# A selective-scan and attention block: when its weights are loaded, and when its scans begin

## The chip, the cores and the metric

The kernel runs on one core of a Trainium2 chip. The metric is device time in microseconds of one execution, the median of three runs. PE is TensorE (matmuls and transposes), DVE VectorE, ACT ScalarE, POOL GpSimd. SP is SyncE; it issues every transfer of this kernel, one after the other, from one in-order queue. Each engine works through its own instruction list in order and waits at an instruction until what it needs is there.

## The reference

Eight images of 64 x 64 positions and 96 channels go through two layers. The first normalises the image in groups of channels, projects it to 2 x 192 channels, convolves one half with 3 x 3 taps per channel, and scans it along two families of diagonals, forwards and backwards (four directions), with 16 states per channel:

```
xz = x @ in_proj_w.T;  xh, z = split(xz)
xc = silu(depthwise_conv3x3(xh) + conv_b)
xs = stack([xc[diag], xc[anti], xc[diag] reversed, xc[anti] reversed])
dts, B, C = split(x_proj_weight @ xs)
delta = softplus(dt_projs_weight @ dts + dt_projs_bias)
A = -exp(A_logs)
h = h * exp(delta * A) + (delta * u) * B      # one step per position
y = h . C + Ds * u
out = layernorm(y) * silu(z) @ out_proj_w.T
```

The second layer adds an attention without a softmax (so that keys times values can be summed first) and a two-layer perceptron whose operands are rounded to an 8-bit float. The decay `A` comes from `A_logs`, one logarithm for each direction, channel and state: 4 x 192 x 16 numbers.

## The kernel before, in words

`weights` loads and prepares all weights. The convolution and the projection before it are folded into one set of weights `wf`: the half of `w_in` is transposed on PE, multiplied by each of nine taps on DVE, transposed back on PE and copied into `wf` (lines 154 to 168, twice nine taps). `a_neg` holds the decays with channels on the partitions: line 145 fetches each run of eight channels transposed, out of an array that has eight channels times 16 states on 128 partitions, 96 transfers in all. `wx` and `ws` (lines 130, 136, 138) hold the weights of B, C and delta, in small pieces; `skip`, `pick` and `xb` are constants built on DVE. The rest serves the later layers. All this stands before `run`.

`run` prepares an image and scans it. Preparing has these parts:

- `measures` (line 379): eight chunks `xt` are loaded (`fetched`, line 366), turned on PE (line 375), and their statistics taken on DVE (line 389); an aggregate follows.
- `front` (line 425): `norm` loads and turns the chunks again and writes the normalised image `xp` on ACT; `convolve` makes each of eight pieces with four or five times 9 matmuls on PE (line 493; the trace has two records for each) and z with two more (line 500), applies silu on ACT and stores `gate` and `image` (lines 512 and 519). Then `walk` (line 529) reads each of eight pieces of the scan order out of `image` with 12 transfers (`ut`, line 538), turns them on PE (line 545), copies them on ACT (line 547) and stores them as `seq` (line 550, two transfers). Three walks run at a time.
- `bring` (line 897) loads a piece `u` of `seq`, and `prologue` (line 820) computes from it delta, delta times u, and B and C, in a chain over PE, ACT, POOL, DVE and PE again (lines 835 to 893). The rows of C go to DRAM (`crow`, line 851) and come back broadcast (`cc`, line 914).

Then the scan loop runs: 8 images x 16 pieces x 16 states = 2048 steps. A step is a decay on ACT (line 923), a feed made on ACT or DVE and PE (lines 937, 945, 947, 962), three scans on DVE (line 958), a product with C on POOL (line 979) and sums on PE (line 993). Line 974 copies the carry once per step.

Beside the loop a planner (`Work`, line 225) lays other work into it. Jobs are Python generators that yield the engine they want and an estimated time; in each step `at` lets jobs go on as far as a credit per engine allows. `SPIN` is a yield that costs nothing and lasts one round. `finish` (line 326) lays down rounds of jobs alone, without a credit, until a condition holds. Jobs need PSUM banks: two are always theirs, and the three `feed` banks as well while no scan runs. All of this decides the order of instructions at build time; nothing of it runs on the chip.

For image 0 the order was: weights; `measures(0)`, `front(0)` and `measures(1)` alone until all are done (line 1065); two `bring`; `prologue(0)` alone; then the loop. At step 5 of image b the planner finishes what is left alone, and then starts `between(b)`, which is `front(b + 1)` and the end layers of image b - 1; at step 128 it starts `measures(b + 2)`.

Of the kernel before, what the change touches and what calls it, by code (L numbers as in the profile page):

```python
# [17 lines left out]
P = 128  # L18
HH = WW = 64
L = HH * WW  # L20
DM = 96
# [29 lines left out]
@with_exitstack  # L51
def hybrid_block(ctx, tc, x, out, w):


    nc = tc.nc
    NB = x.shape[0]
    const = ctx.enter_context(tc.tile_pool(name="const", bufs=1))
    dram = ctx.enter_context(tc.tile_pool(name="dram", bufs=4, space=DRAM))
    k = weights(tc, const, w)
    pool = ctx.enter_context(tc.tile_pool(name="scan", bufs=1))  # L60
    psum = ctx.enter_context(tc.tile_pool(name="psum", bufs=1, space=PSUM))
    with tc.manual_schedule():

        k.tables = lambda: nc.scalar.preload_act_table_set("natural_log_exp_and_others")
        run(tc, pool, psum, dram, x, out, k, NB)


def weights(tc, const, w):


    nc = tc.nc
# [8 lines left out]

    k = SimpleNamespace()
    k.ident = load("ident", [P, P], w["c_ident"])
    k.group = load("group", [DM, DM], w["c_group"])
    k.heads = load("heads", [DM, DM], w["c_heads"])
    k.last = load("last", [1, DM + 1], w["c_last"])
    k.w_in = load("w_in", [DM, 2 * DI], w["w_in"])
    k.w_kv = load("w_kv", [DM + 1, 2 * DM], w["w_kv"])
    k.w_qT = load("w_qT", [DM, DM + 1], w["w_qT"])
    k.w_ff = load("w_ff", [DM, DM], w["w_ff"])
    k.b_ff = load("b_ff", [1, DM], w["b_ff"])  # L90
    k.eps = tile("eps", [P, 1])
    nc.vector.memset(k.eps, 1e-5)
    k.one = tile("one", [P, 1])
# [10 lines left out]
    k.w2q = tile("w2q", [P, 3, DM], F8)  # L104
    k.b1q = tile("b1q", [P, 3])
    k.b2q = tile("b2q", [P, 4, DM])
    nc.gpsimd.memset(k.wf, 0.0)
    nc.gpsimd.memset(k.wx, 0.0)
    nc.gpsimd.memset(k.ws, 0.0)

    k.pick = tile("pick", [NX, FEED.count("D"), P])
    for j, n in enumerate(n for n in range(NS) if FEED[n] == "D"):
        for d in range(2):
            at = XB + d * NS + n
            nc.vector.tensor_copy(
                k.pick[:, j, d * GC : (d + 1) * GC], k.ident[0:NX, at : at + 1].to_broadcast([NX, GC])
            )

    nc.vector.tensor_copy(k.xb, k.ident[0:NX, 2 * NR : 2 * NR + 1])
    with nc.allow_non_contiguous_dma(reason="weights, once"), tc.tile_pool(  # L120
        name="prep", bufs=1
    ) as prep, tc.tile_pool(name="prep2", bufs=2) as prep2, tc.tile_pool(
        name="prepp", bufs=2, space=PSUM
    ) as pp:
        dd = tile("dd", [P, 2, G], pool=prep)
        for d in range(2):
            for g, a, lo, hi, at in PIECES:
                rows = slice(d * GC + at, d * GC + at + hi - lo)
                for first, n, name in ((0, NR, "w_dt"), (XB, NS, "w_b"), (XC, NS, "w_c")):
                    nc.sync.dma_start(  # L130
                        out=k.wx[rows, :, g, first + d * n : first + (d + 1) * n], in_=w[name][lo:hi, a, d::2, :]
                    )
                nc.sync.dma_start(out=dd[rows, :, g], in_=w["ds"][lo:hi, a, d::2])
                for q in range(2):
                    bias = w["b_step"][lo:hi, 2 * q + d, a : a + 1].rearrange("i o -> o i")
                    nc.sync.dma_start(out=k.ws[2 * NR : 2 * NR + 1, q, g, rows], in_=bias)
            for q in range(2):
                nc.sync.dma_start(
                    out=k.ws[d * NR : (d + 1) * NR, q, :, d * GC : (d + 1) * GC],
                    in_=w["w_step"][:, 2 * q + d, :].rearrange("r (g i) -> r g i", i=GC),  # L140
                )
                logs = w["a_logs"][:, 2 * q + d, :].rearrange("(i n) j -> j i n", n=NS)
                for j in range(NJ):
                    lo = d * GC + j % (GC // DPT) * DPT
                    nc.sync.dma_start(out=k.a_neg[lo : lo + DPT, q, j // (GC // DPT), :], in_=logs[j])
        nc.scalar.activation(k.a_neg, k.a_neg, AF.Exp)
        nc.vector.tensor_scalar(k.a_neg, k.a_neg, -1.0, None, ALU.mult)

        both = tile("both", [P, G], pool=prep)
        nc.vector.tensor_tensor(both, dd[:, 0, :], dd[:, 1, :], ALU.add)  # L150
        for g in range(G):
            nc.vector.tensor_scalar(k.skip[:, g, :], k.ident, both[:, g : g + 1], None, ALU.mult)

        conv_w = load("conv_w", [HC, 2, 9], w["conv_w"], pool=prep)
        for a in range(2):
            nc.sync.dma_start(
                out=k.wf[DM : DM + 1, 4, a * HC : (a + 1) * HC], in_=w["conv_b"][:, a : a + 1].rearrange("p o -> o p")
            )
            ps = pp.tile([HC, DM], F32, tag="ps", name="ps")
            nc.tensor.transpose(ps, k.w_in[:, a * HC : (a + 1) * HC], k.ident[:DM, :DM])  # L160
            turned = prep2.tile([HC, DM], F32, tag="turned", name="turned")
            nc.vector.tensor_copy(turned, ps)
            for i in range(9):
                tap = prep2.tile([HC, DM], F32, tag="tap", name="tap")
                nc.vector.tensor_scalar(tap, turned, conv_w[:, a, i : i + 1], None, ALU.mult)
                ps = pp.tile([DM, HC], F32, tag="ps", name="ps")
                nc.tensor.transpose(ps, tap, k.ident[:HC, :HC])
                nc.vector.tensor_copy(k.wf[0:DM, i, a * HC : (a + 1) * HC], ps)

        w_out = load("w_out", [HC, 2, DM], w["w_out"], pool=prep)  # L170
        ln_w = load("ln_w", [HC, 2], w["ln_w"], pool=prep)
        ln_b = load("ln_b", [HC, 2], w["ln_b"], pool=prep)
        for a in range(2):
            nc.vector.tensor_scalar(k.w_ln[:, a, :], w_out[:, a, :], ln_w[:, a : a + 1], None, ALU.mult)
            nc.vector.tensor_scalar(k.b_ln[:, a, :], w_out[:, a, :], ln_b[:, a : a + 1], None, ALU.mult)

        s = load("w1s", [DM, HID], w["w1"], pool=prep)
        nc.vector.tensor_copy(k.w1q, s, saturate=False)
        s = load("w2s", [P, 3, DM], w["w2"], pool=prep)
        nc.vector.tensor_copy(k.w2q, s, saturate=False)  # L180
        s = load("b1s", [P, 3], w["b1"], pool=prep)
        s8 = tile("b1e", [P, 3], F8, prep)
        nc.vector.tensor_copy(s8, s, saturate=False)
        nc.vector.tensor_copy(k.b1q, s8)
        s = tile("b2s", [P, 4, DM], pool=prep)
        nc.sync.dma_start(out=s, in_=w["b2"].unsqueeze(1).to_broadcast([P, 4, DM]))
        s8 = tile("b2e", [P, 4, DM], F8, prep)
        nc.vector.tensor_copy(s8, s, saturate=False)
        nc.vector.tensor_copy(k.b2q, s8)
    return k  # L190


# [32 lines left out]
class Work:  # L225
# [6 lines left out]
    def __init__(self, banks):  # L232
        self.now = 0
        self.alone = False
        self.urgent, self.jobs, self.streams = [], [], []
        self.free = [(b, -9) for b in banks]
        self.long = []
        self.credit = dict.fromkeys(self.PLACES, 0.0)

# [19 lines left out]
    def bank_for(self, j, place):  # L259
        if j not in self.urgent and not self.alone:  # L260
            if any(u.tag == "P" and u.bank for u in self.urgent) or j.bank == "long" and self.long:
                return None
        for i, (b, when) in enumerate(self.free):
            if when < self.now or place == 2 or self.alone:
                if j.bank == "long":
                    self.long.append(b)
                return self.free.pop(i)[0]
        return None
# [513 lines left out]
def run(tc, pool, psum, dram, x, out, w, NB):  # L782
# [269 lines left out]

    def first():
        yield from before(0)
        yield from begin(0)
        if NB > 1:
            yield from before(1)

    def all_done():
        return not (work.streams or work.jobs)  # L1060
# [1 line left out]

    w.tables()
    work.stream(first())
    work.finish(all_done)
    for m in range(2):
        bring(m)
    work.start(prologue(0), urgent=True)
    work.finish(lambda: not work.urgent)
    work.free = [f for f in work.free if any(f[0] is b for b in banks)]  # L1070

    work.start(prologue(1), urgent=True)
# [14 lines left out]
    for i in range(total + LAG + 1):  # L1087
        m, n = divmod(i, NS)
        b, at = divmod(i, PER)
        if i < total:  # L1090
            if at == LAG + 1:
                work.finish(all_done)
                work.stream(between(b))
            if at == PER // 2 and b + 2 < NB:
# [28 lines left out]
            fetch(i + 4)  # L1123
        feeds.pop(i, None)
    work.free += [(f, -9) for f in feed]
    work.stream(end(NB - 1))
    work.finish(all_done)

# [76 lines left out]
```

## Time and profile before

| what | value |
|---|---|
| median of three runs | 12146.02 us (12140.42 to 12148.66) |
| profiled execution, its time | 12157.04 us |
| its span, first to last instruction | 12155.1 us |
| PE, DVE, ACT, POOL busy | 82%, 80%, 78%, 80% |
| DMA queue of SP: packets, MB | 1137510, 1201.51 |
| first carry copy of the first step | 449.38 us after the start |
| 256 steps of image 0, from first carry to first carry | 1296.8 us |
| the same for image 1 | 1447.7 us |

Times in the timeline count from the start of the span. A row of it gives the start, the busy time, the engine, the line, the operation, the tile written and the tiles read, and the number of instructions merged into the row; in brackets the idle time before it and what ended it. SPq rows are issues of transfers, so their duration is the time of issue, waits between the merged ones included, and not that of the data. In the rows of windows each engine has its busy time and instruction count, then come the clock that PE was granted, the busy share of the DMA engines and GB/s.

### The profile page before, as it was taken

Reading aid. Unit: us, or ns where it says so; the run is one execution under the profiler, and the core shown is the slowest. Engines: PE = TensorE matmul, PEld = TensorE weight load, DVE = VectorE, ACT = ScalarE, POOL = GpSimd, SP = SyncE. Lnnn points to the kernel's source line nnn. Section 1 sums busy time; section 2 is a strip of 40 time slices with the busy share of each in tenths; the row PEclk is TensorE's granted clock in tenths of the full one; section 3 lists DMA queues with packets and bytes.
Section 4 is the critical chain, followed back from the end, with each engine's and each line's share of the span. In section 5 each row is a group of like instructions: output and inputs, shape, how many; then the busy total and the mean of one; then the engine's idle time right before and its main releaser. Section 6 shows DMA issues by size and latency. Waiting matters only on the chain.

```text
span 12155.1 us, 187007 instructions
## 1 busy us (share of the span) xinstructions
PE 9958.7 (82%) x62804; PEld 8012.1 (66%) x62804; DVE 9683.1 (80%) x11092; ACT 9501.2 (78%) x19842; POOL 9737.6 (80%) x6927
## 2 busy tenths in 40 slices
PE   4698889888898888988888888988889888888874
PEld 3476667666676666766677666766667666666653
DVE  1488998878888888888888888888888878888971
ACT  1588888877888788877888878887788878878862
POOL 0588998878988788888888889888898888889972
PEclk9799999998998989989899999999989899988985
DMA  2334333533335433353333433344333443322331
GB/s 53 91 92 124 100 93 94 136 104 96 94 88 134 112 94 93 90 141 101 95 90 106 127 102 95 90 127 117 92 92 93 132 108 93 100 87 84 100 93 42
DMA packets 1138471, 1213.47 MB, mean 100 GB/s; under 512 B 464998, under 2 KB 744167, under 8 KB 1137511
## 3 DMA queue, kind: packets, MB, share of 16 engines
q1 hardware_dynamic: 1137510, 1201.51, 36.0%
q8 instruction: 499, 8.18, 0.3%
q14 instruction: 462, 3.78, 0.1%
HBM read 877.94 MB, written 323.09 MB: 99 GB/s over the span
## 4 chain that ended last, share of the span: by engine, by line
PE 29%; ACT 22%; DVE 20%; POOL 11%; issue 9%; SPq 4%; DMA 4%; DVEq 0%; POOLq 0%; ACTq 0%
DVE h L958 13%; ACT feedT L937 8%; PE y L993 7%; PE feed L945 7%; ACT decay L923 6%; POOL h L979 6%; DVE feed L962 4%; PE bank L493 3%; DMA cc<-crow 2%; PE bank L835 2%; SPq L538 2%; PE bank L877 1%; POOL delta L874 1%; PE feed L947 1%; PE bank L858 1%
## 5 line engine op out<-in xcount | busy, mean ns | idle before, releaser
L979 POOL TENSOR_TENSOR h<-h,cc 128x1536 f32<-128x1536 f32 x2048 | 7073.1, 3454 | 401.7 <-DMA cc<-crow 205.0
L958 DVE TENSOR_TENSOR_SCAN h<-decay,carry,feed 128x512 f32<-128x512 f32 x5376 | 6500.6, 1261 | 623.0 <-PE feed L945 510.4
L923 ACT ACTIVATE decay<-delta,a_neg 128x512 f32<-128x512 f32 x6144 | 3976.8, 713 | 1303.6 <-DVE h L958 1298.1
L945 PE MATMUL feed<-ident,feedT 128*128 128x128 f32 x15360 | 2738.5, 303 | 1508.3 <-DVE h L958 1237.9
L993 PE MATMUL y<-ident,h 128*128 128x128 f32 x24576 | 3804.4, 289 | 68.6 <-ACT ys L1021 37.3
L937 ACT ACTIVATE feedT<-duT,rows 128x192 f32<-128x192 f32 x10240 | 3670.8, 443 | 1.6 <-PE feed L945 1.1
L993 PEld LDWEIGHTS y<-ident,h 128*128 128x128 f32 x24576 | 3154.2, 151 | 527.5 <-issue 483.4
L945 PEld LDWEIGHTS feed<-ident,feedT 128*128 128x128 f32 x15360 | 1970.4, 155 | 2118.5 <-DVE h L958 667.9
L962 DVE TENSOR_TENSOR feed<-feed,du 128x512 f32<-128x512 f32 x2304 | 1442.5, 687 | 210.7 <-PE feed L947 205.8
L974 POOL COPY carry<-h 128x3 f32<-128x3 f32 x2048 | 395.4, 193 | 1065.4 <-DVE h L958 985.8
L958 DVE TENSOR_TENSOR_SCAN h<-decay,feed 128x512 f32<-128x512 f32 x768 | 883.9, 1202 | 102.5 <-PE feed L945 83.2
L493 PE MATMUL bank<-wf,xp 97*128 97x192 f32 x4320 | 873.6, 334 | 1.7 <-ACT xp L458 1.7
L947 PE MATMUL feed<-x,pick 77*128 77x512 f32 x1536 | 846.4, 633 | 0.7
L493 PEld LDWEIGHTS bank<-wf,xp 97*128 97x128 f32 x4320 | 704.8, 195 | 28.8 <-issue 15.9
L879 DVE SCALAR_TENSOR_TENSOR delta<-bank,delta 128x512 f32<-128x512 f32 x381 | 258.5, 678 | 287.0 <-POOL delta L874 159.6
L886 POOL TENSOR_TENSOR du<-delta,u 128x1536 f32<-128x1536 f32 x128 | 449.4, 3511 | 10.6 <-DVE delta L879 10.6
L877 PE MATMUL bank<-x,ws 13*128 13x512 f32 x762 | 439.4, 657 | 20.8 <-DVE delta L879 20.8
L872 POOL TENSOR_TENSOR e<-e,duT 128x1536 f32<-128x1536 f32 x128 | 441.9, 3452 | 16.7 <-ACT delta L865 16.6
L858 PE MATMUL bank<-x,ws 13*128 13x512 f32 x766 | 436.6, 650 | 17.3 <-ACT x L848 17.3
L874 POOL TENSOR_TENSOR delta<-delta,e 128x1536 f32<-128x1536 f32 x128 | 441.0, 3446 | 0.1
L947 PEld LDWEIGHTS feed<-x,pick 77*128 77x128 f32 x1536 | 261.0, 201 | 152.7 <-issue 96.2
L835 PE MATMUL bank<-wx,u 128*128 128x77 f32 x3048 | 356.5, 273 | 0.0
(260 smaller groups left out, 8885.1 us busy)
## 6 DMA issues: line engine op xcount, KB each, us to landing
cc<-crow SPq DMA_DIRECT2D x4096, 128.0 KB
u<-seq SPq DMA_DIRECT2D x256, 384.0 KB
wide<-ys SPq DMA_DIRECT2D x512, 192.0 KB
ut<-image SPq DMA_DIRECT2D x768, 64.0 KB
seq<-us SPq DMA_DIRECT2D x128, 384.0 KB
part<-ys SPq DMA_DIRECT2D x64, 768.0 KB
y<-part SPq DMA_DIRECT2D x64, 768.0 KB
y<-wide SPq DMA_DIRECT2D x256, 192.0 KB
```

The lines of the kernel that those rows point to most:

```text
L493: nc.tensor.matmul(v[:, j, :], flat[:, o : o + P], k.wf[:, i, :], start=(i == 0), stop=(i == 8), skip_group_check=True)
L835: nc.tensor.matmul(v[:, j, :], u[:, g, j * P : (j + 1) * P], w.wx[:, q, g, :], start=(g == 0), stop=(g == G - 1))
L874: nc.gpsimd.tensor_tensor(delta, delta, e, ALU.add)
L877: nc.tensor.matmul(ps, w.ws[:, q, g, :], x[0 : 2 * NR + 1, :], start=True, stop=True)
L923: nc.scalar.activation(decays[i][:, g, :], made[m].delta[:, g, :], AF.Exp, scale=w.a_neg[:, q, g, n : n + 1])
L937: nc.scalar.activation(f[part], o.duT[part], AF.Copy, scale=scale)
L945: nc.tensor.transpose(feed[g][:, j * P : (j + 1) * P], feeds[i][:, j * G + g, :], w.ident)
L947: nc.tensor.matmul(feed[0], w.pick[:, FEED[:n].count("D"), :], made[m].x, start=True, stop=True)
L958: nc.vector.tensor_tensor_scan(h[:, g, back], a[:, g, back], feed[g][:, back], init, ALU.mult, ALU.add)
L962: nc.vector.tensor_tensor(feed[g], feed[0], made[m].du[:, g, :], ALU.mult)
L979: nc.gpsimd.tensor_tensor(hs[i], hs[i], c.unsqueeze(1).to_broadcast([P, G, T]), ALU.mult)
L993: nc.tensor.matmul(y[:, j, :], hs[i][:, g, r * P : (r + 1) * P], w.ident, is_transpose=True, start=(n == 0 and j % 4 == 0), stop=(n == NS ...
```

## The change

The loads and products that the convolution needs (`ident`, `w_in`, `conv_w`, `group`, `conv_b`, the 18 taps) come first. All other weights become generators: `loads` (weights of the scans), `layers` (weights of the end layers), and a plain function `rest` (constants). `loads` and `layers` run as one job, which starts after `measures(0)` and yields between groups. The logarithms are loaded as one contiguous tile, transposed once on PE, copied on ACT, written to DRAM and read back in 12 transfers. Some scratch tiles move to the permanent pool.

The scans no longer wait for all of image 0. The stream of image 0 is extended by `between(0)`, and `finish` ends when the end layers' weights are loaded and pieces 0 and 1 of the image are walked. What is left of the stream goes on as jobs: beside `prologue(0)`, in a second `finish` that waits until the three feed banks are free (`kept` keeps jobs from taking them), and in the loop. The start of `between` at step 5 falls away for image 0.

```diff
     k.ident = load("ident", [P, P], w["c_ident"])
+    k.w_in = load("w_in", [DM, 2 * DI], w["w_in"])
+    k.conv_w = load("conv_w", [HC, 2, 9], w["conv_w"])
     k.group = load("group", [DM, DM], w["c_group"])
-    k.heads = load("heads", [DM, DM], w["c_heads"])
...
+    logs = tile("logs", [P, ND, NJ])
+    turned = tile("turned", [ND * NJ, P])
+
+    def loads():
+
+        nc.sync.dma_start(out=logs, in_=w["a_logs"])
         for d in range(2):
             for g, a, lo, hi, at in PIECES:
...
+                if g:
+                    yield SPIN
             for q in range(2):
...
-                logs = w["a_logs"][:, 2 * q + d, :].rearrange("(i n) j -> j i n", n=NS)
-                for j in range(NJ):
-                    lo = d * GC + j % (GC // DPT) * DPT
-                    nc.sync.dma_start(out=k.a_neg[lo : lo + DPT, q, j // (GC // DPT), :], in_=logs[j])
+        ps = yield bank(0.2, 3)
+        v = view(ps, ND * NJ, P)
+        nc.tensor.transpose(v, logs.rearrange("p k j -> p (k j)"), k.ident)
+        yield act(0.4)
+        nc.scalar.copy(turned, v)
+        k.release(ps)
+        rows = dram.tile([ND * NJ, P], F32, tag="logs", name="logs")
+        nc.sync.dma_start(out=rows, in_=turned)
+        yield SPIN
+        for q in range(2):
+            for d in range(2):
+                for g in range(G):
+                    j = (2 * q + d) * NJ + g * (GC // DPT)
+                    nc.sync.dma_start(
+                        out=k.a_neg[d * GC : (d + 1) * GC, q, g, :],
+                        in_=rows[j : j + GC // DPT, :].rearrange("j (i n) -> (j i) n", n=NS),
+                    )
+            yield SPIN
+
+    def rest():
         nc.scalar.activation(k.a_neg, k.a_neg, AF.Exp)
         nc.vector.tensor_scalar(k.a_neg, k.a_neg, -1.0, None, ALU.mult)
...
+    def layers():
+
+        k.heads = load("heads", [DM, DM], w["c_heads"])
...
+        yield SPIN
+        with tc.tile_pool(name="prep", bufs=1, side="right") as prep:
+            w_out = load("w_out", [HC, 2, DM], w["w_out"], pool=prep)
...
+            b2s = tile("b2s", [P, 4, DM], pool=prep)
+            nc.sync.dma_start(out=b2s, in_=w["b2"].unsqueeze(1).to_broadcast([P, 4, DM]))
+            for _ in range(2):
+                yield SPIN
...
     def first():
         yield from before(0)
+        work.start(rest())
         yield from begin(0)
         if NB > 1:
             yield from before(1)
+        yield from between(0)
+
+    w.release = work.release
+
+    def rest():
+
+        with nc.allow_non_contiguous_dma(reason="weights, once"):
+            yield from w.loads()
+            yield from w.layers()
...
     work.stream(first())
-    work.finish(all_done)
+    work.finish(lambda: w.loaded and {0, 1} <= image(0).walked)
+    w.rest()
     for m in range(2):
         bring(m)
     work.start(prologue(0), urgent=True)
     work.finish(lambda: not work.urgent)
+
+    work.kept = feed
+    work.finish(lambda: all(any(f is x for x, _ in work.free) for f in feed))
...
-            if at == LAG + 1:
+            if at == LAG + 1 and b:
                 work.finish(all_done)
                 work.stream(between(b))
...
     work.free += [(f, -9) for f in feed]
+    work.kept = []
```

More of the change, by code (lines that the diff above doesn't have):

```diff
@@ L58, in hybrid_block @@
     dram = ctx.enter_context(tc.tile_pool(name="dram", bufs=4, space=DRAM))
-    k = weights(tc, const, w)
+    k = weights(tc, const, dram, w)
     pool = ctx.enter_context(tc.tile_pool(name="scan", bufs=1))
@@ L65, in hybrid_block, with weights @@
         run(tc, pool, psum, dram, x, out, k, NB)
-def weights(tc, const, w):
+def weights(tc, const, dram, w):
     nc = tc.nc
@@ L82, in weights @@
     k.ident = load("ident", [P, P], w["c_ident"])
+    k.w_in = load("w_in", [DM, 2 * DI], w["w_in"])
+    k.conv_w = load("conv_w", [HC, 2, 9], w["conv_w"])
     k.group = load("group", [DM, DM], w["c_group"])
-    k.heads = load("heads", [DM, DM], w["c_heads"])
[L85 to L90, printed above, removed]
     k.eps = tile("eps", [P, 1])
@@ L106, in weights @@
     k.b2q = tile("b2q", [P, 4, DM])
+    k.pick = tile("pick", [NX, FEED.count("D"), P])
     nc.gpsimd.memset(k.wf, 0.0)
@@ L109, in weights @@
     nc.gpsimd.memset(k.ws, 0.0)
[L111 to L116, printed above, removed]
-            )
[L119 to L125, printed above, removed]
+    with nc.allow_non_contiguous_dma(reason="weights, once"), tc.tile_pool(
+        name="prep2", bufs=2
+    ) as prep2, tc.tile_pool(name="prepp", bufs=2, space=PSUM) as pp:
+        for a in range(2):
+            nc.sync.dma_start(
+                out=k.wf[DM : DM + 1, 4, a * HC : (a + 1) * HC], in_=w["conv_b"][:, a : a + 1].rearrange("p o -> o p")
+            )
+            ps = pp.tile([HC, DM], F32, tag="ps", name="ps")
+            nc.tensor.transpose(ps, k.w_in[:, a * HC : (a + 1) * HC], k.ident[:DM, :DM])
+            turned = prep2.tile([HC, DM], F32, tag="turned", name="turned")
+            nc.vector.tensor_copy(turned, ps)
+            for i in range(9):
+                tap = prep2.tile([HC, DM], F32, tag="tap", name="tap")
+                nc.vector.tensor_scalar(tap, turned, k.conv_w[:, a, i : i + 1], None, ALU.mult)
+                ps = pp.tile([DM, HC], F32, tag="ps", name="ps")
+                nc.tensor.transpose(ps, tap, k.ident[:HC, :HC])
+                nc.vector.tensor_copy(k.wf[0:DM, i, a * HC : (a + 1) * HC], ps)
+    dd = tile("dd", [P, 2, G])
+    both = tile("both", [P, G])
+    logs = tile("logs", [P, ND, NJ])
+    turned = tile("turned", [ND * NJ, P])
+    def loads():
+        nc.sync.dma_start(out=logs, in_=w["a_logs"])
         for d in range(2):
@@ L141, in weights @@
                 )
-                logs = w["a_logs"][:, 2 * q + d, :].rearrange("(i n) j -> j i n", n=NS)
-                for j in range(NJ):
-                    lo = d * GC + j % (GC // DPT) * DPT
-                    nc.sync.dma_start(out=k.a_neg[lo : lo + DPT, q, j // (GC // DPT), :], in_=logs[j])
+        ps = yield bank(0.2, 3)
[11 more added lines that the diff above has]
+                    j = (2 * q + d) * NJ + g * (GC // DPT)
+                    nc.sync.dma_start(
+                        out=k.a_neg[d * GC : (d + 1) * GC, q, g, :],
[3 more added lines that the diff above has]
+    def rest():
         nc.scalar.activation(k.a_neg, k.a_neg, AF.Exp)
         nc.vector.tensor_scalar(k.a_neg, k.a_neg, -1.0, None, ALU.mult)
-        both = tile("both", [P, G], pool=prep)
         nc.vector.tensor_tensor(both, dd[:, 0, :], dd[:, 1, :], ALU.add)
@@ L152, in weights @@
             nc.vector.tensor_scalar(k.skip[:, g, :], k.ident, both[:, g : g + 1], None, ALU.mult)
[L154 to L188, printed above, removed]
@@ L189, in weights @@
-        nc.vector.tensor_copy(k.b2q, s8)
+        for j, n in enumerate(n for n in range(NS) if FEED[n] == "D"):
+            for d in range(2):
+                at = XB + d * NS + n
+                nc.vector.tensor_copy(
+                    k.pick[:, j, d * GC : (d + 1) * GC], k.ident[0:NX, at : at + 1].to_broadcast([NX, GC])
+                )
+        nc.vector.tensor_copy(k.xb, k.ident[0:NX, 2 * NR : 2 * NR + 1])
+    def layers():
+        k.heads = load("heads", [DM, DM], w["c_heads"])
+        k.last = load("last", [1, DM + 1], w["c_last"])
+        k.w_kv = load("w_kv", [DM + 1, 2 * DM], w["w_kv"])
+        k.w_qT = load("w_qT", [DM, DM + 1], w["w_qT"])
+        k.w_ff = load("w_ff", [DM, DM], w["w_ff"])
+        k.b_ff = load("b_ff", [1, DM], w["b_ff"])
+        yield SPIN
+        with tc.tile_pool(name="prep", bufs=1, side="right") as prep:
+            w_out = load("w_out", [HC, 2, DM], w["w_out"], pool=prep)
+            ln_w = load("ln_w", [HC, 2], w["ln_w"], pool=prep)
+            ln_b = load("ln_b", [HC, 2], w["ln_b"], pool=prep)
+            for _ in range(2):
+                yield SPIN
+            for a in range(2):
+                nc.vector.tensor_scalar(k.w_ln[:, a, :], w_out[:, a, :], ln_w[:, a : a + 1], None, ALU.mult)
+                nc.vector.tensor_scalar(k.b_ln[:, a, :], w_out[:, a, :], ln_b[:, a : a + 1], None, ALU.mult)
+        with tc.tile_pool(name="prep", bufs=1, side="right") as prep:
+            w1s = load("w1s", [DM, HID], w["w1"], pool=prep)
+            w2s = load("w2s", [P, 3, DM], w["w2"], pool=prep)
+            b1s = load("b1s", [P, 3], w["b1"], pool=prep)
+            b2s = tile("b2s", [P, 4, DM], pool=prep)
+            nc.sync.dma_start(out=b2s, in_=w["b2"].unsqueeze(1).to_broadcast([P, 4, DM]))
+            for _ in range(2):
+                yield SPIN
+            nc.vector.tensor_copy(k.w1q, w1s, saturate=False)
+            nc.vector.tensor_copy(k.w2q, w2s, saturate=False)
+            s8 = tile("b1e", [P, 3], F8, prep)
+            nc.vector.tensor_copy(s8, b1s, saturate=False)
+            nc.vector.tensor_copy(k.b1q, s8)
+            s8 = tile("b2e", [P, 4, DM], F8, prep)
+            nc.vector.tensor_copy(s8, b2s, saturate=False)
+            nc.vector.tensor_copy(k.b2q, s8)
+        k.loaded = True
@@ L190, in weights @@
+    k.loads, k.rest, k.layers, k.loaded = loads, rest, layers, False
     return k
@@ L236, in __init__ @@
         self.free = [(b, -9) for b in banks]
+        self.kept = []
         self.long = []
@@ L263, in bank_for @@
         for i, (b, when) in enumerate(self.free):
+            if any(b is x for x in self.kept):
+                continue
             if when < self.now or place == 2 or self.alone:
```

## The prediction

> **What bounds the kernel now.** I read the page's head first, then busy time in 50 us windows of the start, then the merged timeline of the same stretch, then the starts of the carry copies (line 974), which number the scan steps.
>
> ```profile
> span 12155.1 us, 187007 instructions
> PE 9958.7 (82%) x62804; PEld 8012.1 (66%) x62804; DVE 9683.1 (80%) x11092; ACT 9501.2 (78%) x19842; POOL 9737.6 (80%) x6927
> ```
>
> Four engines at about 80% over the span: a balanced scan loop. The change does not edit a step of it; it edits what lies before it. There the windows (columns PE, PEld, DVE, ACT, POOL busy, PE clock, DMA share, GB/s) look different:
>
> ```profile
> 0.00:50.00 50.00, 0.37 (x1) 0.16 (x1) 2.22 (x16) 1.28 (x1) 2.88 (x7) 1.00 0.12 11
> 50.00:100.00 50.00, 0.00 (x0) 0.00 (x0) 0.84 (x4) 0.00 (x0) 0.00 (x0) 1.00 0.09 2
> 150.00:200.00 50.00, 49.07 (x267) 45.48 (x268) 7.47 (x12) 14.33 (x14) 0.01 (x1) 1.00 0.20 56
> 300.00:350.00 50.00, 11.70 (x64) 10.54 (x64) 0.00 (x0) 8.70 (x16) 0.00 (x0) 0.57 0.46 109
> 350.00:400.00 50.00, 11.66 (x51) 8.96 (x52) 4.17 (x6) 3.42 (x6) 0.00 (x0) 0.57 0.57 140
> ```
>
> For 100 us nobody computes; then PE is full (convolution); then PE has a quarter of the time. The timeline gives the reason and my anchors:
>
> ```profile
> 20.99 17.34 SPq L145 DMA_DIRECT2D a_neg<-in_a_logs  x24
> 108.70 0.44 DVE L165 TENSOR_SCALAR tap<-turned,conv_w 96x96 f32<-96x96 f32 x2
> 119.09 0.36 DVE L188 CAST b2e<-b2s 128x384 fp8e5<-128x384 f32 x1 [4.13 <-DMA b2s<-in_b]
> 123.73 24.37 SPq L368 DMA_DIRECT2D xt<-in_x  x13
> 150.06 14.71 PE L493 MATMUL feed<-wf,xp 97*128 97x192 f32 x72 [2.36 <-POOL xp L444]
> 281.16 23.95 SPq L538 DMA_DIRECT2D ut<-image  x36
> 318.14 25.39 SPq L538 DMA_DIRECT2D ut<-image  x36
> 356.10 17.61 SPq L538 DMA_DIRECT2D ut<-image  x24
> 382.85 15.49 SPq L368 DMA_DIRECT2D xt<-in_x  x8
> 405.19 5.37 PE L835 MATMUL feed<-wx,u 128*128 128x77 f32 x24
> 445.87 6.78 DVE L958 TENSOR_TENSOR_SCAN h<-decay,feed 128x512 f32<-128x512 f32 x6
> ```
>
> Until 108.7 SP is the bound: it issues weights, among them 4 x 24 transfers of decay logarithms. 150 to 268 is PE (8 pieces of 14 us). 281 to 399 is SP again: 96 walk loads at 0.66 us, then 8 loads for the second image's statistics. From 405 the first prologue (a chain over PE, ACT, POOL) leads to the first scan at **445.9**. All I predict is where that first scan goes, and what the loop of image 0 pays for it.
>
> **The change, part by part.** I use the order of the changed kernel's instructions on each engine (known without running it) and durations of the rows above.
>
> *Weights first.* SP issued the first tap's inputs after everything else; now w_in and conv_w are its second and third transfers. In the trace w_in is issued at 2.49 and its transpose runs at 4.74; issued at 1.2 it gives the turned copy by 4.1, so the first tap stands at 4.2 instead of 108.7. The 18 taps took 108.70 to 123.73 = 15.0 us; 4.2 of it is DVE standing on the b2s load (third row), which has left the queue: 10.8. The first xt, which waits for the last tap, moves from 123.7 to 15.0: **-108.7**. Of this, 96 logarithm transfers at 0.717 us (17.2 per 24) are 68.9, replaced by 1 + 1 + 12. The Trainium skill, "DMA: Bandwidth & Descriptors" (Anatomy of one DMA), states about 2 us fixed per DMA; 96 of those one after another would be 192 us, more than the whole stretch lasted. The row decides: issue is paced at 0.72 and landings overlap.
>
> *Weights between the sections.* Their SP time now stands beside the statistics and the convolution. Before the norm's loads come 15 transfers; 14 of these took 6.5 us in the trace (10.07 to 16.52), so about 7. The norm's first load was issued near 136.7 and used at 142.99; 7 us later it lands about 4 late, and the third piece's load, which waits for the first piece's transposes, ends near 151.5 where POOL's memset of xp let the convolution go at 150.06: **+1.5**. In the convolution a piece has 14 us of PE; SP needs 0.6 (gate) + 7 (12 image writes) + at most 9 transfers x 0.5 = 12.1: covered. Were it not, each extra us per piece would cost up to 8. Before the first gate (168.3 in the trace, so near 61) SP has 45 weight loads, 22 us, and is through at about 57. Turning the logarithms costs one PE transpose and one ACT copy in the ACT queue ahead of a norm: **+0.5**. Their round through DRAM is three pieces ahead of its use; cost nothing. Behind the last image writes come w1, w2, b1, b2. Issue (1.9) fits under the writes' landing (279.3 to 281.2), but SP keeps eight transfers in flight, so the eighth walk load waits for b2s, which took 7.8 us to land (111.25 to 119.06): issued 1.4 after the last write it lands at 9.2, where that walk load would go at 1.9 + 7 x 0.66 = 6.5: **+2.7**. From there on the walk stands at -104.0.
>
> *Scans begin with two pieces.* Naively six walks and the statistics leave the path. The order says otherwise: three walks run together, so pieces 0 to 2 finish at once, and while the first prologue is laid down all queued jobs go on beside it. On SP, behind the four u loads stand 36 walk loads, then crow, 6 stores, 24 walk loads, 4 stores, 6 xt, and only then cc. On PE the prologue's matmuls alternate with walks 3 to 7 and six statistics chunks. So:
> - u behind seq: the first walks' stores must have landed before u is read, with 36 walk loads queued behind on SP. The same page puts most of the 2 us down to the write's receipt, which speaks against the change; the trace's store-free loads land in 2.3 to 2.5. I take 2 + 4 x 0.64 = **+4.4** (0 to 5).
> - Walks 3 to 5 end at 344.1 - 104.0 + 4.4 = 244. Prologue matmuls between them (1.1 + 0.9 + 2) and crow delay the stores: **+4.4**. The last walks' loads end at 374.3 - 104.0 + 8.8 = **279**.
> - L877's matmuls stand behind walk 7: transposes 1.1 + 1.7, then 5.3 for the three (same as 418.25), 1.7 for the walks' rest: 289. DVE 0.7; POOL du 3.4: 293. POOL's other four passes (9.8 us, 420.7 to 430.7) are hidden below the wait for walk 7; uncovered they would show whole.
> - The du transposes stand between xt chunks, and xt has two buffers: SP waits for PE, each load lands 2.5 later. Three such rounds: du at 297, the third at 303, second prologue's matmuls 3, rows, pick 2, feed 2: first scan at about **312** (306 to 317).
>
> Before 445.9, so -134. Deferred to the loop: two statistics chunks and an aggregate, PE 2.1 + 1: +2. Constants for k.rest (12 picks 1.8, skip 0.7, exp 0.3) lie under the seq landing.
>
> *Image 0's loop.* Starts of the first carry of each 16 steps give 89.8, 79.9, 92.4, 80.5, 87.8, 91.7, 90.1 while image 1 is convolved and walked, then 74 to 78. The floor is 75.3, so preparing image 1 costs 612 - 527 = 85 us. It now begins some 8 steps later (last gate at step 101 instead of 93, last walk at 129 instead of 120, of 256): the same work, other alignment, 0 +- 10. From about step 130 on both kernels have the same order.
>
> Sum: -134 + 2 = **-132** on a profiled 12157.0 (span 12155.1, 1.9 around it), hence 12025; the runs' median was 12146.0, 11 lower: **12014**.
>
> **Rivals.**
> 1. *Only the weights pay.* Walks and prologue interleave so badly that the second part returns nothing: xt rounds and cold PE eat it. For: the order above. Against: the old chain had 405 to 436 behind the walks, most of it now beside them. Gain 104 + 0: 12042; with ten us of loop alignment 12052.
> 2. *The six walks really leave the path.* First scan 41 us after u lands (216): 257, gain 189 - 20 for walks in the loop: 11977. Against: PE is in order and walk 7's transposes precede L877.
> 3. *Slower: image 1 is not ready.* At step 5 of image 1 everything left is finished alone. Serial convolution and walks took 150 to 382 = 232 us against 85 hidden; if none of it had started by then, -132 + 147 = +15: 12161. It decides once about 90% is left over. The order puts the last walk at step 129 of 256.
> 4. *No change*: the weights stay the bound, SP issuing the same transfers before the walks. Against: 82 transfers are gone, and 12 of 14 us per piece fit.
>
> **How the numbers follow.** The case above 0.72, rival 1 0.15, rival 2 0.08, rival 3 0.02, rival 4 0.03. Range 11988 to 12048: low from the early ends of u and xt rounds (-8), loop -10 and part of rival 2; high takes in rival 1's 12042 and some. A change under 0.2% (24 us) cannot be told from none here. Faster 0.95 (the first three), same 0.03, slower 0.02.
>
> **What would show it.** In the trace after: first xt near 15; convolution near 43; first walk load near 177; prologue's first matmul near 216, but L877's successor near 283 behind the last walk; first scan near 312; sixteen-step times of image 0 summing to 1297 +- 12, image 1 1448 as before. Wrong if SP leaves gaps on PE between convolution pieces, if the walks' loads slow below 0.66 us each, or if image 1's sum moves.

## The result, and the profile after

The median of four runs each fell from 12143.22 us (12137.30 to 12148.66) to **12014.52 us** (12012.80 to 12028.16): 129 us less, a ratio of 0.9897 with a 95% interval of 0.9879 to 0.9914. The forecast was 12014, faster, in a range of 11988 to 12048.

The head of the page of the changed kernel, and then its windows of the start (columns as before: PE, PEld, DVE, ACT, POOL busy, PE clock, DMA share, GB/s):

```profile
span 12013.6 us, 186895 instructions
PE 9964.7 (83%) x62805; PEld 8013.1 (67%) x62805; DVE 9683.0 (81%) x11092; ACT 9500.1 (79%) x19843; POOL 9739.2 (81%) x6927
```

```profile
0.00:50.00 50.00, 24.43 (x100) 17.82 (x101) 13.78 (x49) 5.70 (x9) 9.12 (x23) 1.00 0.23 52
50.00:100.00 50.00, 49.13 (x285) 45.18 (x284) 8.52 (x14) 14.59 (x15) 0.00 (x0) 1.00 0.33 88
200.00:250.00 50.00, 18.52 (x92) 16.46 (x93) 2.24 (x18) 9.57 (x18) 0.00 (x0) 0.59 0.54 129
250.00:300.00 50.00, 18.99 (x69) 11.55 (x68) 4.85 (x7) 10.54 (x16) 13.20 (x5) 0.59 0.52 134
```

Busy time is what it was, engine by engine; the work is the same. PE, which had one matmul in the first 100 us, convolves from 43.6 on. What has not gone is the thin stretch of walks: between 200 and 300 PE is busy for 37.5 us of 100. The merged timeline of the changed kernel has the anchors:

```profile
4.43 0.45 DVE L122 TENSOR_SCALAR tap<-turned,conv_w 96x96 f32<-96x96 f32 x2
15.23 12.83 SPq L411 DMA_DIRECT2D xt<-in_x  x8
43.63 13.06 PE L536 MATMUL feed<-wf,xp 97*128 97x192 f32 x72
172.52 26.69 SPq L581 DMA_DIRECT2D ut<-image  x36
211.97 4.49 SPq L947 DMA_DIRECT2D u<-seq  x4
216.50 26.58 SPq L581 DMA_DIRECT2D ut<-image  x36
220.59 5.37 PE L878 MATMUL feed<-wx,u 128*128 128x77 f32 x24 [15.91 <-DMA u<-seq]
276.30 1.09 PE L588 MATMUL feed<-ident,ut 128*128 128x128 f32 x4 [6.89 <-DMA ut<-image]
287.56 3.42 POOL L929 TENSOR_TENSOR du<-delta,u 128x1536 f32<-128x1536 f32 x1 [22.93 <-DVE delta L922]
301.21 2.80 PE L878 MATMUL bank<-wx,u 128*128 128x77 f32 x24
308.18 6.77 DVE L1001 TENSOR_TENSOR_SCAN h<-decay,feed 128x512 f32<-128x512 f32 x6
```

From the first prologue matmul to the first scan it took 40.7 us before (405.2 to 445.9) and now takes 87.6. The prologue begins 185 us earlier and ends 138 earlier. Between its parts now stand walks 3 to 7 and six chunks of the second image's statistics; the experiments below take apart what they cost.

| anchor | before | forecast | measured |
|---|---|---|---|
| first load of an image | 123.7 | 15.0 | 15.23 |
| convolution begins | 150.1 | 43 | 43.63 |
| first 36 walk loads issued | 305.1 | 201.1 | 199.2 |
| first prologue's first matmul | 405.2 | 216 | 220.6 |
| first transposes of walk 7 | 374.3 | 279 | 276.3 |
| du done | 436.2 | 293 | 291.0 |
| first scan | 445.9 | 312 | 308.2 |
| 256 steps of image 0 | 1296.8 | 1299 | 1294.0 |
| span | 12155.1 | 12023 | 12013.6 |

Images 1 to 7 and the end took 10408.9 us before and 10407.9 after.

### The profile page after: what moved, and what is told of

The parts are those of the page before. It is cut to its first block, busy times and chain, and to the rows that moved or that the text cites. A ratio compares the mean times of both kernels' runs of the same rounds, so it can differ in the third digit from the quotient of the medians.

```text
span 12013.6 us, 186895 instructions
## 1 busy us (share of the span) xinstructions
PE 9964.7 (83%) x62805; PEld 8013.1 (67%) x62805; DVE 9683.0 (81%) x11092; ACT 9500.1 (79%) x19843; POOL 9739.2 (81%) x6927
## 4 chain that ended last, share of the span: by engine, by line
PE 30%; ACT 20%; DVE 20%; POOL 12%; issue 9%; DMA 4%; SPq 3%; DVEq 0%; POOLq 0%; ACTq 0%
DVE h L1001 13%; ACT feedT L980 8%; PE y L1036 7%; PE feed L988 7%; POOL h L1022 7%; ACT decay L966 6%; DVE feed L1005 4%; PE bank L536 3%; DMA cc<-crow 2%; PE bank L878 2%; SPq L581 2%; POOL delta L917 1%; PE bank L920 1%; PE feed L990 1%; PE bank L901 1%
## 5 line engine op out<-in xcount | busy, mean ns | idle before, releaser
L920 PE MATMUL bank<-x,ws 13*128 13x512 f32 x766 | 444.9, 661 | 17.6 <-DVE delta L922 17.6
L912 POOL TENSOR_SCALAR duT<-e 128x1536 f32<-128x1536 f32 x128 | 193.9, 1514 | 227.8 <-ACT e L905 227.8
```

The source lines that it names most:

```text
L920: nc.tensor.matmul(ps, w.ws[:, q, g, :], x[0 : 2 * NR + 1, :], start=True, stop=True)
```

## The experiments

The theory after the result: the weights move everything up to the walks by some 106 us, and the early scans add only about 30, since the first prologue stands among walks 3 to 7 on PE and SP. The rivals: only the weights pay; the walks have left the path; the loop takes back what is deferred to it. In what follows "first scan" is the start of the first row of scans, and "loop of image 0" the time from the first carry copy to that of step 256. Both are read from one trace of each kernel. The loops of the changed kernel and of two that differ from it only before the walks took 1294.0, 1294.9 and 1296.1 us, so a difference of 2 us in a loop says nothing. Times are compared by their ratio to the kernel before, run beside each.

**The weights alone.**

```diff
     def first():
...
-        yield from between(0)
...
-    work.finish(lambda: w.loaded and {0, 1} <= image(0).walked)
+    work.finish(all_done)
...
-            if at == LAG + 1 and b:
+            if at == LAG + 1:
```

> The weights part of the change alone; the scans wait for all of image 0 and for the second image's statistics, as before. My theory (the weights give about -106 to the first walk load, the early scans only some -30 more): first scan near 445.9 - 106 = 340, time 106 below the kernel before, 12037. Rival, only the weights pay: the same time as the changed kernel, 12014.

12053.09 us against 12149.66 for the kernel before beside it: ratio 0.9921 (0.9906 to 0.9936), 97 us; 106 was forecast, and the two profiled executions lie 109 apart. First scan at 340.95, loop of image 0 1297.0. The place of the first scan is right to 1 us. The interval touches that of the changed kernel (up to 0.9914), so the time alone does not put the rival out; the first scan does, which the second part moves on to 308.2 at a loop of 1294.0.

**The early scans alone**, on the weights of before:

```diff
         if NB > 1:
             yield from before(1)
+        yield from between(0)
...
-    work.finish(all_done)
+    work.finish(lambda: {0, 1} <= image(0).walked)
...
+    work.kept = feed
+    work.finish(lambda: all(any(f is x for x, _ in work.free) for f in feed))
...
-            if at == LAG + 1:
+            if at == LAG + 1 and b:
...
```

> The early scans alone, on the weights of the kernel before. My theory: first scan 30 to 34 earlier, near 414, time about 12112. Rival, only the weights pay: no difference, 12143. Rival, six walks leave the path: some 130 earlier at the first scan, time about 12030.

12124.65 us against 12149.66: ratio 0.9980 (0.9973 to 0.9986), 25 us. First scan at 416.7, 29 earlier, loop 1298.5. The second part does pay (the interval leaves out 1), but less than a quarter of the 130 us that six walks and eight statistics chunks off the path would give. 97 + 25 = 122 stands beside 129 for both; the parts add, within what the runs spread.

**Walks 3 to 7 held back** until the loop's first feeds are laid down, on the changed kernel:

```diff
-        yield [walk(c) for c in range(NST)], 3
+        def held():
+            while at.held:
+                yield SPIN
+
+        if at.held:
+            yield [walk(c) for c in range(3)], 3
+            yield [held()], 1
+            yield [walk(c) for c in range(3, NST)], 3
+        else:
+            yield [walk(c) for c in range(NST)], 3
...
+                held=(b == 0),
...
     PER = NSTEP * NS
+    image(0).held = False
```

> The changed kernel with walks 3 to 7 and all behind them held back until the loop's first feeds are laid down. My theory (the first prologue stands behind walks 3 to 7 on PE and SP): its matmuls start at 220 as now, and the chain of 40.7 us that it took before brings the first scan near 261 instead of 308; the loop of image 0 pays for five walks and 36 loads in one lump on SP, +10 to +25 over 1294; time 11975 to 11995. Rival, the loop takes back all of it: 12014.

**11973.12 us**, ratio 0.9860 (0.9843 to 0.9876): faster than the changed kernel, whose interval ends at 0.9879. In the timeline of this kernel the prologue has nothing between its parts:

```profile
211.63 4.55 SPq L957 DMA_DIRECT2D u<-seq  x4
220.30 5.37 PE L888 MATMUL feed<-wx,u 128*128 128x77 f32 x24 [15.92 <-DMA u<-seq]
251.42 2.82 PE L944 MATMUL feed<-ident,du 128*128 128x128 f32 x12 [12.73 <-POOL du L939]
264.75 2.33 DVE L1011 TENSOR_TENSOR_SCAN h<-decay,feed 128x512 f32<-128x512 f32 x2
```

It starts where it did (220.3) and needs 44.5 us and not 87.6. So the interleaving is the cause of 43 us, shown by taking it away. The loop of image 0 rises from 1294.0 to 1303.3: the five walks and the statistics cost 9 us there. First scan and loop together are 34 us better. The profiled executions lie 53 us apart; the other 19 stand in images 1 to 7, which the edit does not touch, and are spread between executions.

POOL waits for the broadcast rows of C (`cc`) more than before. The lists of who waited for whom, within the loop of image 0 (columns: waited for, us in total, times, longest), have one line each, for the kernel before, the changed kernel and this one:

```profile
POOL h L979 <- DMA cc<-crow: 26.3, 4, 12.8
```

```profile
POOL h L1022 <- DMA cc<-crow: 1.8, 1, 1.8
```

```profile
POOL h L1032 <- DMA cc<-crow: 31.4, 7, 12.8
```

Only two of the seven waits, 2.3 us at 299.1 and 2.5 us at 341.5, fall among the held walks. The longest ends at 1043.7, behind the loads of image 1's first three walks:

```profile
1014.88 24.27 SPq L581 DMA_DIRECT2D ut<-image  x36
1039.25 0.56 SPq L411 DMA_DIRECT2D xt<-in_x  x1
1039.90 1.10 SPq L967 DMA_DIRECT2D cc<-crow  x2
```

For 24 us, some five steps, SP issues walk loads and no `cc`. The kernel before has the same lump of 36 and the same wait of 12.8 us at step 98. So these waits are in the main a matter of image 1's walks, and the 9 us that this loop pays can't be put down to the lump of the held ones.

**The held walks one at a time**, so that SP gets 12 loads and not 36 in a lump:

```diff
-            yield [walk(c) for c in range(3, NST)], 3
+            yield [walk(c) for c in range(3, NST)], 1
```

> As the kernel that holds walks 3 to 7, but these go into the loop one at a time, so that SP gets 12 walk loads in a lump and not 36. The first scan stays at 265. If the lump of 36 is what cost the loop of image 0 its 9 us over 1294, this returns to about 1295 and the time is 8 below, near 11965; if it is the walks' own PE and ACT work, the loop stays near 1303 and the time near 11973.

Neither. 11996.96 us, ratio 0.9869 (0.9853 to 0.9884), whose interval overlaps that of the kernel with walks in threes; but the loop took 1324.0 us, 21 more. The first four groups of 16 steps took 76.4, 75.4, 76.6 and 76.2, near the floor of 75.3, and no wait for `cc` is left in them. POOL's waits for `cc` fell from 31.4 to 20.6 us, but 9.3 came to the carry copies, and the longest (19.0 us) again stands behind 36 walk loads of image 1. The cost came later: with the walks drawn out to step 41, image 1's first gate stands at step 92 (73 with walks in threes) and its last walk at 193 (168); steps 128 to 191 took 91.6, 90.1, 97.9 and 85.2 per 16, against 92.4, 93.8, 77.6 and 75.9.

**The third image's statistics later**, on that kernel:

```diff
-            if at == PER // 2 and b + 2 < NB:
+            if at == (PER // 2 if b else PER * 13 // 16) and b + 2 < NB:
```

> The kernel that lets the held walks go one at a time, with the third image's statistics started at step 208 of image 0 in place of 128, when image 1 is walked. Its loop of image 0 took 1324 us against 1303 with the walks in threes. If the 21 us come from the statistics running beside the convolution of image 1, the loop returns to 1303 to 1308 and the time falls by about 18. If they come from convolving beside the backward pieces themselves (steps 128 on have more work of their own), the loop stays near 1324 and the time near that of the kernel it is made from.

Between the two: loop 1316.5, so 7.5 of the 21 us, by one trace each; the times (11986.35 us, ratio 0.9867 from 0.9853 to 0.9882) do not tell the two apart. With the statistics gone from beside it, preparing image 1 in steps 128 to 191 still takes 91.6, 89.8, 89.3 and 84.6. That the backward pieces leave less room would fit the other 13; no run took that cause away, and it is open.

**Only the second image's statistics held back**; the walks stay in the prologue:

```diff
     def first():
...
+        def held():
+            while image(0).held:
+                yield SPIN
+
+        yield [held()], 1
         if NB > 1:
             yield from before(1)
...
```

> The changed kernel with only the second image's statistics held back until the loop's first feeds are laid down; walks 3 to 7 stay beside the first prologue. It costs the xt rounds alone. My theory (the prologue's last transposes stand between xt chunks that wait for two buffers): first scan 6 to 8 earlier, near 301, time near 12007. Rival, the walks alone make the delay: first scan stays at 308, time 12014.

First scan at 304.52, though its prologue began 2.5 us later (223.10): from there to the scan 81.4 us in place of 87.6, so the xt rounds (the loads of chunks that stand between the prologue's last transposes) cost 6.2. The time is 12012.24, ratio 0.9882 (0.9864 to 0.9900): the same as the changed kernel. The loop took 1299.0, 5 more: about what left the prologue came back there.

**Two walks ahead, the rest one at a time**, then **the rest in threes** (the last number below is then 3):

```diff
-            yield [walk(c) for c in range(3)], 3
+            yield [walk(c) for c in range(2)], 2
...
-            yield [walk(c) for c in range(3, NST)], 1
+            yield [walk(c) for c in range(2, NST)], 1
```

> As the kernel that holds the walks and lets them go one at a time, but with only walks 0 and 1 ahead of the prologue. 12 walk loads at 0.66 and 2 stores at 1.25 leave the path: first scan near 254, some 10 below 265; loop of image 0 as in that kernel plus one walk (+1 to +4); time 7 to 10 below that kernel, about 11957 if the lump theory holds. Rival, step 8 stalls because piece 2 is not there: the gain is lost in the first 16 steps.

11984.18 us, ratio 0.9860 (0.9846 to 0.9875). First scan at 255.12, loop 1325.8: 8 us gained, 2 paid, and no stall in the first 16 steps (77.7). The absolute forecast failed with the lump theory that it rested on.

> Walks 0 and 1 alone ahead of the prologue, the rest held and let go three at a time. First scan at 255 as with the other kernel that walks two; the preparation of image 1 starts near step 75 and not 104, so the loop of image 0 should take about 1303 to 1308, not 1326. Time about 8 below the kernel that holds walks 3 to 7: a ratio near 0.985. Rival, the loop takes back whatever the first scan gains: ratio 0.986.

11969.51 us, ratio 0.9853 (0.9837 to 0.9869). The ratio came as forecast, but not by its reason. First scan at 254.02, but the loop took 1315.4 and not 1303 to 1308: first scan and loop together 1569.4, against 1568.1 for the kernel that holds walks 3 to 7. The gain of 11 at the first scan was taken back, though image 1's gates stand at nearly the same steps (75 to 144, 73 to 141); why is open. The two versions can't be told apart by time; both beat the changed kernel.

**The logarithms by 96 transfers**, between the convolution's sections:

```diff
+                logs = w["a_logs"][:, 2 * q + d, :].rearrange("(i n) j -> j i n", n=NS)
+                for j in range(NJ):
+                    lo = d * GC + j % (GC // DPT) * DPT
+                    nc.sync.dma_start(out=k.a_neg[lo : lo + DPT, q, j // (GC // DPT), :], in_=logs[j])
+                yield SPIN
-
-        ps = yield bank(0.2, 3)
...
-            yield SPIN
```

> The changed kernel with the logarithms fetched by 96 transposing transfers as before, in four groups of 24 between the convolution's sections, in place of the turn on PE. My theory (SP has about 29 us of gaps beside the convolution, and 82 more transfers at 0.717 us are 58.8): about 30 us later, first walk load near 202, time 12045 (12039 to 12055). Rival, the place of the transfers alone matters: no difference, 12014. Rival, nothing hides them: +59, 12073.

12057.58 us, ratio 0.9923 (0.9908 to 0.9937): by the ratios some 32 us over the changed kernel, 33 by the spans of the two profiled executions. The intervals touch, so the places in the trace decide: first walk load at 208.98 (36.5 later), first scan at 346.51 (38.3 later). In this kernel's SP rows each group of 24 fills more than a convolution piece, and in the list of waits PE stands twice:

```profile
49.17 17.34 SPq L153 DMA_DIRECT2D a_neg<-in_a_logs  x24
76.81 17.27 SPq L153 DMA_DIRECT2D a_neg<-in_a_logs  x24
134.56 17.70 SPq L153 DMA_DIRECT2D a_neg<-in_a_logs  x24
152.82 17.19 SPq L153 DMA_DIRECT2D a_neg<-in_a_logs  x24
```

```profile
PE feed L518 <- DVE pre L504: 15.4, 1, 15.4
PE feed L400 <- DMA xt<-in_x: 10.4, 1, 10.4
```

DVE could not empty a bank because `pre` was not yet written to the image; `xt` stood behind logarithms. Of 58.8 us of additional issue 22 were hidden, against 29 estimated. Without the turn on PE, moving the weights would have brought the first walk load forward by 72 us and not by 109. In the changed kernel 75 small transfers are issued between the statistics and the last image writes (48 + 4 of the scan weights, 14 of the logarithms, 9 of the end layers): 19 before the convolution begins and 56 beside it. There is room for those, and for few more.

**b2 a piece earlier**, loaded and cast beside w_out:

```diff
             ln_b = load("ln_b", [HC, 2], w["ln_b"], pool=prep)
+            b2s = tile("b2s", [P, 4, DM], pool=prep)
+            nc.sync.dma_start(out=b2s, in_=w["b2"].unsqueeze(1).to_broadcast([P, 4, DM]))
...
             b1s = load("b1s", [P, 3], w["b1"], pool=prep)
-            b2s = tile("b2s", [P, 4, DM], pool=prep)
-            nc.sync.dma_start(out=b2s, in_=w["b2"].unsqueeze(1).to_broadcast([P, 4, DM]))
```

> The changed kernel with the load and the cast of b2 beside those of w_out, a piece of the convolution earlier, and no longer just ahead of the walks. My theory (the eighth walk load waits for b2s): the first 36 walk loads are issued in 24 us in place of 26.7, first scan near 305.5. Rival, the image's own writes slow the first walk loads: 26.7 stays. The time moves less than the runs' spread.

A single execution, 12007.74 us. SP's list of waits in the changed kernel has the first line below for its walk loads; here that line is gone, and the walk loads have the second:

```profile
SPq L581 <- DMA b2s<-in_b: 2.8, 1, 2.8
```

```profile
172.62 23.69 SPq L581 DMA_DIRECT2D ut<-image  x36
```

The loads start at the same time, are issued in 23.7 us in place of 26.7, and the first scan is at 305.63. In the changed kernel seven walk loads go out behind b2s, and the eighth is issued at 180.18, when b2s has landed (180.17). So the wait is that of the eighth load for b2s.

## Why the prediction was right

*Weights first* (-108.7): the first image load moved by 108.5. The taps took 10.8 us without DVE's wait for b2s (4.43 to 15.23). That issue at 0.72 us, and not the skill's 2 us per transfer, was the price of the logarithms is borne out: in the experiment with 96 transfers, 24 of them take 17.2 to 17.7 us. The section that the prediction names describes transfers issued by GpSimd; those of this kernel are all issued by SyncE.

*Weights between the sections* (+1.5, +0.5, +2.7): the convolution began 2.1 us behind the shift of the loads. The count behind the +1.5 was off: 13 transfers and not 15 stand before the norm's loads, and the stretch from 10.07 to 16.52 holds 12 and not 14; the 13 took 7.7 us (28.11 to 35.85), near the 7 assumed. "At most 9 transfers" beside a piece was wrong too: 12 loads of `a_neg` stand in one gap and take 8.3 us, and SP was through 0.5 us before the next gate. Before the first gate stand 39 weight loads and not 45.

The convolution then took 116.2 us (43.63 to 159.84) against 118.9 (150.06 to 268.99); the sum had +0.5 here where -2.7 came. Of it, 1.65 us stand in the first piece, whose first 72 records take 13.06 us (rows of the timeline) and took 14.71. At its start PE's matmuls come 0.32 us apart, later 0.16; the slow ones were 17 before and are 8 now. Another 0.9 is one wait of PE for ACT's norm less (two and not three, 0.87 us each, one of them at the turn of the logarithms). So the first walk load went out at 172.5, and not near 177. b2s cost 2.7 by the difference of the two rows (26.69 - 23.95) and 3.0 by the experiment.

*Scans begin with two pieces.* The naive reading of the diff, rival 2, would have been 11977, and the order of instructions had it right: walk 7 stood before the delta matmuls (its first transposes at 276.30, L920 at 279.02). From the first 36 walk loads to walk 7 the sum had 77.9 us, and 77.1 came; from there to du 14 and 14.7.

The term of u was right on SP and wrong in its reason. SP stood 4.6 us (211.88 to 216.50); 2 + 4 x 0.64 is 4.6 and not the 4.4 written. But the sum let a load land 2.3 to 2.5 us after its issue, which was read from image loads of 192 KB. A load of `u` has 384 KB, and by the trace's semaphores the last three of the four land at 220.45, 222.25 and 224.02, with the DMA engines busy for 0.95 of the time at 217 GB/s (216.0 to 220.5). The prologue's matmul needs the first two and so waited until 220.6, not 216. In the kernel before it also started 4.2 us after the last issue of u. That matmul's delay was hidden, since the prologue's next part stood behind walks 3 to 5 on PE. The landings were not: three walk loads waited for them.

```profile
SPq L581 <- DMA u<-seq: 3.1, 3, 1.2
```

So the walk loads slowed to 0.74 us each, by b2s in the first 36 (in the sum) and by u in the second (not in it). It was one of the prediction's signs of being wrong, and shorter terms elsewhere made up for it. The xt rounds measured 6.2; from du to the first scan the sum had 19 us, and 17.2 came.

*The loop of image 0* (+2, alignment +-10): -2.8, little more than the 2 us by which loops of the same order differ.

*The sum.* The predicted span was 12023, and 12013.6 came: 3.8 from the first scan, 4.8 from the loop, 1.0 from the rest. That the median was hit to 1 us is luck in part: the sum took 11 us off for the way from the profiled execution to the median, as before, and the profiled execution of the changed kernel (12015.44) lies 1 above its median. This and the 10 us of the span cancel.

*The rivals.* "Only the weights pay" is refuted by the second experiment; "image 1 is not ready" never came near, its last walk stood at step 129. "The walks leave the path" is what the kernel with held walks does: 11973 against the 11977 worked out for it. That nearness is luck in part too: its prologue began 4 us later and took 44.5 us in place of 41, the loop cost 9 us in place of 20, and the runs spread by more than what is left.

## What to carry to other kernels

A wait that is relaxed in the source frees only what stands behind it in each engine's order: look where the relaxed work is laid down, and hold back the part that would stand in the new critical chain. Weights that are used late can hide behind a compute-bound section, up to the gaps of the queue that issues them; count those gaps per section, since a burst longer than a section stops the section. A gain at the start that pushes other work later can be paid for there, so sum the start and the loop, not the start alone. And look in the trace when a wait falls before naming its cause: a sum over the loop mixed the waits of the held walks with those of the next image's.

## What was not expected of the hardware

A load of one row of 96 numbers, repeated into 128 partitions four times (b2s, 192 KB), took 8.3 us from issue to the cast that waited for it (171.84 to 180.19), where the thirteen image loads of the same size before the convolution of the kernel before landed 2.4 to 3.2 us after their issue began. It held up a transfer that shares no data with it, the eighth behind it. Four loads of `u`, 384 KB each, landed 1.8 us apart; that they follow stores need not be the reason for their lateness, since they came as late in the kernel before (4.2 us from the last issue to the matmul), where eight image loads stood between the stores and them.
